# Score products of 128 keys as four products of 32 keys in column tiles

## The chip, the cores and the metric

The kernel runs on one core of one Trainium2 chip. The metric is the device time in microseconds (us) of one execution. Before the change it is 1825.35 us, the median of three runs (1824.77 to 1825.51). Engines are named as in the profile: PE is TensorE (its matmuls), PEld its weight loads, DVE is VectorE, ACT is ScalarE, POOL is GpSimd and SP is SyncE.

## The reference

The input is 32 images of 256 channels and 32 x 32 pixels, all fp32. The kernel normalises each group of 8 channels, projects to queries, keys and values (8 heads of 32 channels, 1024 tokens), computes strictly causal attention and adds the input:

```python
q = jnp.einsum('oc,bcs->bos', q_w, xf) + q_b[None, :, None]
kv = jnp.einsum('oc,bcs->bos', kv_w, xf) + kv_b[None, :, None]
k, v = (kv[:, :EMBED_C], kv[:, EMBED_C:])
...
mask = jnp.tril(jnp.ones((S, S), dtype=x.dtype), -int(MASK_CENTER))
scores = jnp.einsum('bhqd,bhkd->bhqk', q, k) / jnp.sqrt(jnp.asarray(dk, x.dtype))
scores = jnp.where(mask == 0, jnp.asarray(-10000.0, x.dtype), scores)
attn = jax.nn.softmax(scores, axis=-1)
attn = jnp.where(mask == 0, jnp.asarray(0.0, x.dtype), attn)
out = jnp.einsum('bhqk,bhkd->bhqd', attn, v)
...
x = x + _L0_conv_ref(_gn(x), L0_conv_q_w, L0_conv_q_b, L0_conv_kv_w, L0_conv_kv_b)
```

## The kernel before

Queries and keys of four heads lie in one tile with the channels on the partitions: head j of a group g has the 32 partitions 32j to 32j + 31 (`live["q", b, g]`, `live["k", b, g]`). Scores are computed transposed, keys on the PSUM partitions and queries along the columns. A product of 128 keys with up to 512 queries therefore has a stationary operand of 32 rows (channels) and 128 columns (keys), and a moving operand of 32 rows and the queries as columns. In the array it fills the row tile of its head, 32 rows by all 128 columns; the four heads lie in four row tiles.

A piece (`piece`, line 265) is one block of 128 keys against one half of the queries (512) for the four heads of a group. A piece on the diagonal is cut: with d = 1 it has two blocks, of 384 and 128 queries; with d = 2 one of 256. A long piece can also be cut into two parts of 256 queries. Each batch element has 12 visits, and a visit pairs a long piece (512 columns for each head, `full`) with a short one (256 columns for each head, `half`). There are 32 batch elements, so 384 visits.

`scores` (line 304) issues one visit. The scores go to three pairs of PSUM banks, `pairs[0]` and `pairs[1]` for heads 0, 1 and 2, 3 of the long piece, and `pairs[2]`, seen as `short`, for all four heads of the short piece, two heads in each of its banks. [...] So the short products of heads 2 and 3 come first (`first`), then the long products of heads 0 to 3, then the short products of heads 0 and 1. The last two wait on a semaphore, `bank_free`, that each product of `first` raises by one at its end; `live["free"]` holds the count to wait for. Then ACT takes three exponentials (lines 342 and 344) from PSUM to SBUF as `e` and `eh`, and POOL masks the diagonal.

`values` (line 356), one visit later, multiplies the values with `e` and `eh`: four matmuls of 128 rows and 32 columns, one for each head, that lie in four column tiles and write 32 PSUM partitions each of `acc`. The projections (`product`, line 152, called by `project_qk` and `project_v`) are cut in the same way into four column tiles of 32 columns.

The order on PE, ACT, DVE and POOL is written out by hand (`tc.manual_schedule`). The main loop (line 611) does for each visit i: the scores of visit i, what is due at i (mostly one projection, `pp` or `ppv`), the values of visit i - 1, and what is due after these (norms, row sums, results). So TensorE alternates between one stage of score products in 32x128 tiles and one stage of projections and values in 128x32 tiles.

In the trace every fp32 product stands as two loads and two matmuls (two passes): the 3584 score products are 7168 matmuls at L283. 256 visits have 8 products (16 passes), 128 have 12 (24 passes, where the long piece has blocks of 384 and 128 queries).

Of the kernel before, what the change touches and what calls it, by code (L numbers as in the profile page):

```python
# [17 lines left out]
P = 128  # L18
HD = 32
CPG = 8  # L20
HALF = 512
# [4 lines left out]
SUM_MAX = 1.0e20  # L26
HALFBANK = HALF // 2
ROW = 64


@with_exitstack
def tile_norm_attention_residual(
# [19 lines left out]
    nc = tc.nc  # L52
# [34 lines left out]
    avg = avg.rearrange("p a b -> p (a b)")  # L87
    in_range = const.tile([P, ROW], F32, name="in_range")
    nc.gpsimd.memset(in_range, 1.0)
# [8 lines left out]
    def unshifted():  # L98
        live = {}
# [178 lines left out]
        def scores_of(pc, pair, j, n=0):  # L278

            b, (g, hf, k, part, blocks) = pc  # L280
            rows = slice(HD * j, HD * (j + 1))
            kb, cols, of = blocks[n]
            return nc.tensor.matmul(  # L283
                pair[:, cols], lhsT=live["k", b, g][rows, kb * P : (kb + 1) * P],
                rhs=live["q", b, g][rows, hf * HALF + of.start : hf * HALF + of.stop],
                start=True, stop=True, skip_group_check=True,
            )

        def mask(pc, e, heads=slice(0, 4)):


            g, hf, k, part, blocks = pc
            if k < hf * BPH:
                return
            n = len(blocks)
            diagonal = e[:, heads, : n * P].rearrange("p j (n q) -> p j n q", q=P)
            nc.gpsimd.affine_select(  # L297
                out=diagonal, in_=diagonal, pattern=[[0, heads.stop - heads.start], [0, n], [1, P]],
                compare_op=ALU.is_gt, fill=0.0, base=0, channel_multiplier=-1,
            )  # L300
            if k == 0:
                nc.gpsimd.memset(e[0:1, heads, 0:1], 1.0)

        def scores(b, full, half):


            tag = "e0" if full[2] == 0 else "e"
            name = f"{b}_{full[0]}_{full[1]}_{full[2]}"
            e = epool.tile([P, 4, HALF], F32, tag=tag, bufs=4 if tag == "e0" else 3, name=f"{tag}_{name}")
            eh = epool.tile([P, 4, HALFBANK], F32, tag="eh", bufs=4, name=f"eh_{name}")  # L310
            pairs = [ps_s.tile([P, 2, HALF], F32, tag="sT", name=f"sT_{name}_{a}") for a in range(3)]
            short = pairs[2].rearrange("p bank (n q) -> p bank n q", n=2)
            last = b == B - 1 and full[:2] == (NG - 1, NH - 1) and half[2] == NB - 2
            short_of = lambda heads, n: [scores_of((b, half), short[:, j % 2, n, :], j) for j in heads]
            long_of = lambda heads, n: [scores_of((b, full), pairs[j // 2][:, j % 2, :], j, n) for j in heads]


            if not last:
                first = short_of((2, 3), 1)
                for n in range(len(full[4])):  # L320
                    long_of(range(4), n)
            else:

                long_of(range(4), 0)
                long_of((0, 1), 1)
                first = short_of((2, 3), 1)
                long_of((2, 3), 1)

            for ins in first:
                ins.then_inc(bank_free, 1)  # L330
                tc.no_tile_sem_insts.add(ins.ins.name)
            live["free"] = live.get("free", 0) + len(first)
            wait = nc.tensor.wait_ge(bank_free, live["free"])
            for ins in first:
                tc.declare_no_dep(wait.ins, ins.ins, reason="the semaphore orders them")
            for j in range(2):
                lo = scores_of((b, half), short[:, j, 0, :], j)
                for ins in first:
                    tc.declare_no_dep(lo.ins, ins.ins, reason="the semaphore orders them")
            for a in range(3):  # L340
                if a == 2:
                    exp = nc.scalar.activation(eh.rearrange("p (n bank) q -> p bank n q", n=2), short, AF.Exp)  # L342
                else:
                    nc.scalar.activation(e[:, 2 * a : 2 * a + 2, :], pairs[a], AF.Exp)  # L344

            for ins in first:
                tc.add_to_no_dep_group(f"first_{name}", ins.ins)
                tc.add_to_no_dep_group("first", ins.ins)
            tc.declare_no_dep(exp.ins, group=f"first_{name}", reason="through the last two products")
            tc.declare_fence(exp.ins, group=f"first_{name}")  # L350
            for heads in (range(2), range(2, 4)) if last else (range(4),):
                mask(full, e, slice(heads.start, heads.stop))
            mask(half, eh)
            live["e", b, full], live["e", b, half] = e, eh
# [46 lines left out]
        def sum_folded(b, heads):  # L401
            if heads.start == 0:
                live["rows", b] = small.tile([P, ROW], F32, tag="rows", name=f"rows_{b}")
            for j in heads:
# [32 lines left out]
        def check(rows, least, most):  # L437
            nc.vector.scalar_tensor_tensor(in_range, rows, least, in_range, ALU.is_ge, ALU.mult)
            nc.vector.scalar_tensor_tensor(in_range, rows, most, in_range, ALU.is_le, ALU.mult)

        def invert(b):
            rows = live["rows", b]
            check(rows, SUM_MIN, SUM_MAX)
            inv = small.tile([P, ROW], F32, tag="inv", name=f"inv_{b}")
            nc.vector.reciprocal(inv, rows)
            turned = small.tile([P, ROW], F32, tag="inv_turned", name=f"inv_turned_{b}")
            nc.vector.transpose(turned, inv)
# [94 lines left out]
        with tc.manual_schedule(engines={ENG.PE, ENG.Activation, ENG.DVE, ENG.Pool}):  # L542
# [36 lines left out]
            for b in range(B):  # L579
                first, last = b * N, b == B - 1  # L580
# [30 lines left out]
            for i in range(B * N + 1):  # L611
                if i < B * N:
                    scores(i // N, *visits[i % N])
                for f in at.pop(i, ()):
                    f()
                pcs = products[(i - 1) % N] if i else ()
                if i == B * N:

                    sums(3, pcs, False)
                for pc in pcs:  # L620
                    values((i - 1) // N, pc, i <= (B - 1) * N or pc not in by_pe)
                if i == B * N - 2:

                    sums(3, [None, *pcs])
                if i == B * N - 1:
                    sums(3, pcs)
                for f in after.pop(i, ()):
                    f()
# [172 lines left out]
```

## Time and profile before

| What | us |
|---|---|
| median of three runs | 1825.35 |
| span of the profiled execution | 1823.5 |
| PE busy with matmuls | 1811.0 (99%) |
| DVE busy | 1654.1 (91%) |
| ACT busy | 1479.1 (81%) |
| PE busy at score products, 256 columns, 3072 of 400 ns | 498.5 |
| the same, 512 columns, 2048 of 613 ns | 395.6 |
| the same, 384 columns, 1024 of 507 ns | 170.7 |
| the same, 128 columns, 1024 of 269 ns | 98.9 |
| weight loads of score products, 7168 of 184 ns | 444.3 |

The profile is of one execution. Busy time is the union of what an engine does at one time; matmuls overlap, so the rows of shapes overlap too and their sum is above what the score stages take. The means of matmuls contain the way through the array and, at the head of a stage, the wait for the first weights. A matmul's end is modelled by the profiler; its start is recorded. The granted TensorE clock is 0.998 of the full one over the span.

In a line of a group stand: source line, engine and operation, what it writes and reads, its shape (32*128 is 32 rows and 128 columns of the array, 32x256 the moving operand), how often, and then busy us and mean ns. In a line of the timeline the first two numbers are the start and the length in us of a run of such instructions. In a line of waits stand the total in us, the number of waits and the longest.

### The profile page before, as it was taken

To read this page: it belongs to the slowest core of one execution; us is meant where nothing else is said; L and a number is where in the kernel's file an instruction comes from. 1 tells how busy PE (TensorE), PEld (TensorE's weight loads), DVE (VectorE), ACT (ScalarE), POOL (GpSimd) and SP (SyncE) were. 2 spreads that over 40 slices of the span, in tenths; PEclk is the share of its full clock that TensorE was granted. 3 is DMA by queue.
4 is the path that set the end of the run, shared out by engine and by line. 5 is a ranking of instruction groups with operands and counts; after the bars stand their busy time and mean duration, and the time that the engine had idled before them with its cause. 6 is when DMAs were issued, how large, how long until landed. Compare 5 with 4: busy or idle time off the path is not lost.

```text
span 1823.5 us, 53762 instructions
## 1 busy us (share of the span) xinstructions
PE 1811.0 (99%) x23220; PEld 926.4 (51%) x23220; DVE 1654.1 (91%) x1762; ACT 1479.1 (81%) x1860; POOL 800.4 (44%) x774
## 2 busy tenths in 40 slices
PE   9999999999999999999999999999999999999997
PEld 5454555555554555555555545555455555555543
DVE  4699999999999999999999999999999999999988
ACT  6888878888788888788887888877888878888785
POOL 1553544534534445344354353443444544535432
PEclk9999999999999999999999999999999999999999
DMA  3456676676776676767767767667667676676662
GB/s 122 74 98 136 132 148 115 131 152 119 146 131 123 139 132 134 151 111 135 139 133 144 120 129 149 123 140 137 127 133 135 131 152 114 127 151 124 123 123 73
DMA packets 77780, 234.99 MB, mean 129 GB/s; under 512 B 20320, under 2 KB 21344, under 8 KB 61664
## 3 DMA queue, kind: packets, MB, share of 16 engines
q0 software_dynamic: 15872, 97.53, 39.9%
q1 hardware_dynamic: 61664, 133.96, 26.5%
q8 instruction: 183, 3.00, 0.7%
q14 instruction: 61, 0.50, 0.1%
HBM read 66.85 MB, written 34.57 MB: 56 GB/s over the span
## 4 chain that ended last, share of the span: by engine, by line
PE 99%; DVE 0%; DMA 0%; ACT 0%; issue 0%
PE sT L283 32%; PE acc L369 27%; PE pp L157 26%; PE ppv L157 13%; PE pd L414 1%; DMA x<-in_x_dram 0%; PE pv L157 0%; DVE st L167 0%; PE pm L157 0%; ACT e L344 0%; PE wt L136 0%; DVE rb_last L480 0%; ACT eh L342 0%; DVE rb_last L470 0%; DVE turned L467 0%
## 5 line engine op out<-in xcount | busy, mean ns | idle before, releaser
L344 ACT ACTIVATE e<-sT 128x1024 f32<-128x1024 f32 x768 | 744.9, 1022 | 272.9 <-PE sT L283 219.0
L377 DVE TENSOR_TENSOR e<-e,e 128x1536 f32<-128x1536 f32 x376 | 631.2, 1679 | 17.7
L377 DVE TENSOR_TENSOR e<-e,eh 128x1024 f32<-128x1024 f32 x380 | 524.3, 1394 | 117.3 <-PE acc L369 97.6
L297 POOL TENSOR_SCALAR_AFFINE_SELECT e<-e 128x512 f32<-128x512 f32 (+1 forms) x257 | 383.2, 1491 | 553.8 <-ACT e L344 550.5
L283 PE MATMUL sT<-q,k 32*128 32x256 f32 (+3 forms) x7168 | 606.4, 458 | 0.0
L283 PEld LDWEIGHTS sT<-q,k 32*128 32x128 f32 x7168 | 444.3, 184 | 153.0 <-ACT eh L342 65.0
L157 PE MATMUL pp<-xn,wT 128*32 128x512 f32 x4096 | 492.2, 598 | 0.1
L369 PE MATMUL acc<-e,v 128*32 128x512 f32 (+2 forms) x4096 | 400.6, 486 | 0.0
L342 ACT ACTIVATE eh<-sT 128x1024 f32<-128x1024 f32 x384 | 396.7, 1033 | 0.0
L393 POOL DMA_DIRECT2D e<-e x248 | 201.8, 820 | 398.0 <-DMA e<-e 318.5
L157 PE MATMUL ppv<-wT,xn 128*32 128x256 f32 x4096 | 247.5, 382 | 0.0
L369 PEld LDWEIGHTS acc<-e,v 128*32 128x32 f32 x4096 | 132.6, 110 | 223.3 <-issue 192.1
L369 PE MATMUL acc<-eh,v 128*32 128x256 f32 x3072 | 224.4, 379 | 0.0
L157 PEld LDWEIGHTS pp<-xn,wT 128*32 128x32 f32 x4096 | 107.2, 109 | 219.4 <-issue 205.7
L369 PEld LDWEIGHTS acc<-eh,v 128*32 128x32 f32 x3072 | 98.5, 110 | 164.2 <-issue 153.2
L157 PEld LDWEIGHTS ppv<-wT,xn 128*32 128x32 f32 x4096 | 120.4, 109 | 102.7 <-issue 32.4
L297 POOL TENSOR_SCALAR_AFFINE_SELECT eh<-eh 128x512 f32<-128x512 f32 x128 | 167.2, 1306 | 0.4
L223 ACT ACTIVATE xn<-x,shift,rstd 128x512 f32<-128x512 f32 x124 | 103.1, 831 | 0.0
L480 DVE SCALAR_TENSOR_TENSOR rb<-rb,v_bias_col,x 128x512 f32<-128x512 f32 x124 | 93.5, 754 | 4.4
L237 ACT ACTIVATE k<-pp,qk_bias 128x512 f32<-128x512 f32 x128 | 89.6, 700 | 2.2 <-PE pm L157 1.1
L237 ACT ACTIVATE q<-pp,qk_bias 128x512 f32<-128x512 f32 x128 | 89.8, 701 | 1.0 <-PE pp L157 1.0
L406 DVE STREAM_TRANSPOSE turned<-folded 128x512 f32<-128x512 f32 x124 | 87.6, 706 | 2.2
(70 smaller groups left out, 663.3 us busy)
## 6 DMA issues: line engine op xcount, KB each, us to landing
e<-e POOLq DMA_DIRECT2D x124, 512.0 KB, 7.0
x<-in_x_dram SPq DMA_DIRECT2D x64, 512.0 KB, 6.2
e<-e POOLq DMA_DIRECT2D x124, 256.0 KB, 4.6
folded<-e SPq DMA_DIRECT2D x124, 256.0 KB, 4.5
rb<-inverses SPq DMA_DIRECT2D x124, 256.0 KB, 8.0
out_dram<-rb SPq DMA_DIRECT2D x124, 256.0 KB, 4.5
inverses<-inv_turned SPq DMA_DIRECT2D x31, 32.0 KB, 1.7
out_dram<-rb_last SPq DMA_DIRECT2D x3, 256.0 KB, 3.4
```

Source lines behind the costliest of these rows:

```text
L157: nc.tensor.matmul(out[part], lhsT=lhsT[:, part], rhs=rhs, start=start, stop=stop, skip_group_check=True)
L223: nc.scalar.activation(xn, xt, AF.Identity, bias=live["shift", b][:, g : g + 1], scale=rstd)
L237: nc.scalar.activation(live[key][:, cols], pp, AF.Identity, bias=qk_bias[:, n, g : g + 1], scale=(SCALE, 1.0)[n],)
L283: return nc.tensor.matmul(pair[:, cols], lhsT=live["k", b, g][rows, kb * P : (kb + 1) * P], rhs=live["q", b, g][rows, hf * HALF + of.start ...
L297: nc.gpsimd.affine_select(out=diagonal, in_=diagonal, pattern=[[0, heads.stop - heads.start], [0, n], [1, P]], compare_op=ALU.is_gt, fill= ...
L342: exp = nc.scalar.activation(eh.rearrange("p (n bank) q -> p bank n q", n=2), short, AF.Exp)
L344: nc.scalar.activation(e[:, 2 * a : 2 * a + 2, :], pairs[a], AF.Exp)
L369: nc.tensor.matmul(acc[HD * j : HD * (j + 1), of], lhsT=live["v", b][:, kb, h * HD : (h + 1) * HD], rhs=e[:, j, cols], start=first, stop=l ...
L377: nc.vector.tensor_add(total[:, :, of], total[:, :, of], e[:, :, cols])
L393: nc.gpsimd.dma_start(out=total[:rows], in_=total[rows : 2 * rows], accum_op=ALU.add)
L406: nc.vector.transpose(turned, live["folded", b][:, j, :])
L480: nc.vector.scalar_tensor_tensor(rb, rb, v_bias_col[:, g : g + 1], xt[:, g, cols], ALU.add, ALU.add)
```

## The change

Each score product of 128 keys is now four products of 32 keys. The stationary operand of each has 32 rows and 32 columns, and its result goes to 32 PSUM partitions, so it lies in one 32x32 tile of the array: row tile of its head, column tile of its keys. The four read the same queries. `scores_of` returns a list of four instructions in place of one; `short_of` flattens the lists, and `long_of` doesn't use what it gets back. All eight instructions of `first` now raise `bank_free`, and the count waited for grows by eight for each visit. The order of heads is as before, with the four column tiles of a head one behind the other.

```diff
+WIDE = 32
...
             kb, cols, of = blocks[n]
-            return nc.tensor.matmul(
-                pair[:, cols], lhsT=live["k", b, g][rows, kb * P : (kb + 1) * P],
-                rhs=live["q", b, g][rows, hf * HALF + of.start : hf * HALF + of.stop],
-                start=True, stop=True, skip_group_check=True,
-            )
+            return [
+                nc.tensor.matmul(
+                    pair[c : c + WIDE, cols], lhsT=live["k", b, g][rows, kb * P + c : kb * P + c + WIDE],
+                    rhs=live["q", b, g][rows, hf * HALF + of.start : hf * HALF + of.stop],
+                    start=True, stop=True, skip_group_check=True,
+                )
+                for c in range(0, P, WIDE)
+            ]
...
-            short_of = lambda heads, n: [scores_of((b, half), short[:, j % 2, n, :], j) for j in heads]
+            short_of = lambda heads, n: [m for j in heads for m in scores_of((b, half), short[:, j % 2, n, :], j)]
...
             for j in range(2):
-                lo = scores_of((b, half), short[:, j, 0, :], j)
-                for ins in first:
-                    tc.declare_no_dep(lo.ins, ins.ins, reason="the semaphore orders them")
+                for lo in scores_of((b, half), short[:, j, 0, :], j):
+                    for ins in first:
+                        tc.declare_no_dep(lo.ins, ins.ins, reason="the semaphore orders them")
```

## The prediction

> **What bounds the kernel now.** I read the head of the page first, then the chain that ended last, the groups by shape, the timeline of TensorE round one score stage, and single instructions in narrow windows.
>
> ```profile
> span 1823.5 us, 53762 instructions
> PE 1811.0 (99%) x23220; PEld 926.4 (51%) x23220; DVE 1654.1 (91%) x1762; ACT 1479.1 (81%) x1860; POOL 800.4 (44%) x774
> PE 99%; DVE 0%; DMA 0%; ACT 0%; issue 0%
> ```
>
> TensorE is busy 99% of the span and the chain lies on it for 99%. A busy PE is not yet a full one, so the next question is whether it ever waits for another engine. Waits of PE, longest first, in the whole run:
>
> ```profile
> PE pc L497 <- DVE worst L495: 3.5, 1, 3.5
> PE busy L143 <- POOL ident masks.py:199: 1.7, 1, 1.7
> PE pm L157 <- DVE mv L168: 0.6, 1, 0.6
> ```
>
> These belong to the beginning and the end. In between TensorE follows its own order, so what one score stage gains or loses goes one to one into the span. There are 384 such stages (12 visits x 32 batches). One of them in the timeline of the matmuls and of the weight loads:
>
> ```profile
> 904.30 1.05 PE L369 MATMUL acc<-eh,v 128*32 128x256 f32 x16
> 905.27 1.57 PE L283 MATMUL sT<-q,k 32*128 32x256 f32 x16
> 906.78 1.92 PE L157 MATMUL pp<-xn,wT 128*32 128x512 f32 x16
> ...
> 905.27 1.17 PEld L283 LDWEIGHTS sT<-q,k 32*128 32x128 f32 x16 [0.41 <-issue]
> 906.78 0.16 PEld L157 LDWEIGHTS pp<-xn,wT 128*32 128x32 f32 x8 [0.33 <-issue]
> ```
>
> Eight products stand in the trace as sixteen matmuls and sixteen loads: each fp32 product runs as two passes. The stage takes 1.50 us from its first matmul to the first of the next stage. By single starts, the second passes of heads 2 and 3 begin at 905.595, row tiles 2 and 3 take their long products at 905.811 and 906.240: a pass costs 216 ns at 256 columns and 429 at 512. One row tile has a long and a short product, so 2 x 429 + 2 x 216 = 1290 ns. The rest of the 1.50 us is the first weight load, the start lag of the last tile, and 91 ns in which the tile shape changes. The same shape change costs 96 ns on the way in (the last stream of acc ends at 905.179).
>
> How long the first load shows is seen in the modelled length of a matmul right after a shape change against one later in its stage (min/median/max):
>
> ```profile
> L283 PE MATMUL sT<-q,k x2: 478/478/478, 905.3 to 905.3; 32*128 32x256 f32 x2
> L283 PE MATMUL sT<-q,k x6: 374/478/692, 905.3 to 905.6; 32*128 32x256 f32 x4, 32*128 32x512 f32 x2
> L157 PE MATMUL ppv<-wT,xn x8: 379/392/404, 901.7 to 901.9; 128*32 128x256 f32 x8
> ```
>
> 478 - 374 = 104 ns behind a load of 128 columns, 404 - 379 = 25 ns behind one of 32.
>
> The start lag is seen where four loads stand in a row (the first column is the start, 905.273 to 905.293):
>
> ```profile
> 905.27 0.20 PEld L283 LDWEIGHTS sT<-q,k 32*128 32x128 f32 x4 [0.41 <-issue]
> ```
>
> One load lasts 0.18 us and four together 0.20: tiles start 6.7 ns apart. They do so although the second pass of each product stands between them in the program, so TensorE takes work of different tiles out of order.
>
> [...] the trace has 93 (second pass of head 3 starts 905.601, ends after 374 at 905.975, the waiting load starts 906.068). [...]
>
> **The change, part by part.** It turns 3584 score products into 14336, each pass of a 32x128 tile into four of 32x32. The order of stages, the waits and all work on the other engines stay; the waits on exponentials are the same in number.
>
> Streaming: every 32x32 tile still passes the same 768 columns twice, sixteen of them at once in place of four, so 1290 ns stay. No gain here.
>
> First load: 104 ns become 25, so about -80 ns per stage. Loads in the middle are hidden behind matmuls in both.
>
> Start lag: the last of the first-started tiles is now the 16th, 15 x 6.7 = 100 ns behind the first, against 3 x 6.7 = 20 before; +80. It isn't hidden: head 1's column tile 3 must then do its long and its short product, 100 + 25 + 858 + 432 = 1415 ns, against 20 + 104 + 858 + 432 = 1414 before. These two parts cancel.
>
> The counted wait (bank_free): each visit's first products now count 8 in place of 2, and the short products of heads 0 and 1 wait behind them, with the next stage's instructions queued behind. Head 3's last tile starts 7 x 6.7 = 47 ns in, its second pass at 47 + 25 + 216 = 288, ending after 374 at 662. [...] Eight loads follow 6.7 ns apart, the last at 982, and its matmul some 30 later, 1012 (nearest row: after a real wait the mean's product loads at 7.58 and starts at 7.61). Head 1's last tile is free at 100 + 25 + 858 = 983. So +30 ns. Below: 0, if the increments run from the first completion, which is 48 ns earlier. Above: 93 / 2 = 46 ns each, 370 for eight, +127 ns. I take 30: 384 x 0.030 = 11.5 us.
>
> Stages with 24 matmuls (128 of 384, those with a block of 128 columns): now 96 passes and 96 loads. Eight tiles at a time are in such a block, one pass 107 ns, against 8 x 6.7 = 54 ns of starts, and the loads of the others come in between. I take 20 ns (0 to 107, one pass more): 128 x 0.020 = 2.6 us.
>
> Shape changes: still two per visit, 32-row tiles to 128-row tiles and back; 91 and 96 stay. Instruction fetch: 3.00 MB at 0.7% of the DMA engines, not doubling: nothing.
>
> Sum: -80 + 80 + 30 ns, 384 times, and 2.6 us: +14.1 us. The profiled execution spans 1823.5, so 1837.6. The median is 1825.35, 1.85 above that span, so 1839.5, say 1840.
>
> **The rivals.**
>
> Fed too slowly, chance 0.15. TensorE's instructions go from 46,440 to about 89,400; a visit's stage from 32 or 48 to 128 or 192. [...] In the trace before instructions come every 1811 / 46440 = 39 ns without a gap, an upper bound on the feed; the eight passes of the mean product after a real wait (16 instructions in 103 ns, 6.4 each) may have been queued. [...]
>
> Tiles not independent, chance 0.13. The trace shows overlap over four row tiles and over four column tiles, never both. If products of one column tile start in program order, a head's first pass starts with the second pass of the head before, and the stage is 4 x 429 + 4 x 216 + 216 + 45 = 2840 ns, +1.43 x 384 = 549 us: 2374.
>
> Faster, chance 0.28. Place: the first 100 ns of each stage. [...] if none of it lies on the path, 80 ns, 31 us: 1795. It decides as soon as the lag of the last tile is under 80 ns more than now and the counted wait is over by then. For it: the weight load really shrinks by 80 ns. Against it: the 6.7 ns are regular in every stage, and the wait has more increments.
>
> No change, chance 0.12: load and lag cancel and the wait stays hidden, 1825.
>
> **How the numbers follow.** My forecast, slower by about 0.8%, has 0.32; its own range is 1825 to 1825 + 127 x 0.384 + 107 x 0.128 = 1888. Below 1800 lies some 0.07 of the faster case, above 2200 the case of dependent tiles with 0.13; the range is 1800 to 2200. Within 0.2% (3.7 us) is what a measurement here can't tell from no change. Slower: 0.32 + 0.15 + 0.13 = 0.60; faster 0.28; same 0.12.
>
> **What would show it.** The stage's length from first score matmul to next stage: 1.50 now, 1.53 forecast. First matmul 399 ns long (374 + 25). Sixteen starts 6.7 ns apart. The load behind the counted wait about 935 ns into the stage. [...] if heads follow each other, tiles are dependent. A stage under 1.49 makes the forecast wrong, and so does PE waiting for exponentials.

## The result and the profile after

The changed kernel takes 2062.18 us (median of five runs, 2059.06 to 2065.94) against 1825.35 us before: a ratio of 1.13 with a 95% interval of 1.1287 to 1.1312. It is slower, as forecast, but by 13% and not by 0.8%.

The head of the page after the change, with busy time and share of the span for each engine, and the chain that ended last:

```profile
span 2064.2 us, 96826 instructions
PE 2042.5 (99%) x44724; PEld 982.8 (48%) x44724; DVE 1639.9 (79%) x1762; ACT 1488.2 (72%) x1860; POOL 745.4 (36%) x774
PE 98%; issue 1%; DVE 0%; DMA 0%; ACT 0%
```

TensorE is still the bound, and the other engines do the same work in a longer span. What PE waits for (total us, number, longest):

```profile
PE sT L285 <- issue: 9.0, 12, 1.9
PE pc L501 <- DVE worst L499: 3.5, 1, 3.5
```

No wait for exponentials has come in. The first line is new and small; it comes back at the end of this section. Now the timeline of matmuls round one stage of each kind, the smaller and the larger one (start, length, number of matmuls):

```profile
1025.80 1.97 PE L285 MATMUL sT<-q,k 32*32 32x256 f32 x64
1027.69 0.64 PE L158 MATMUL pp<-xn,wT 128*32 128x512 f32 x4
```

```profile
1041.53 2.52 PE L285 MATMUL sT<-q,k 32*32 32x256 f32 x96
1043.98 0.64 PE L158 MATMUL pp<-xn,wT 128*32 128x512 f32 x4
```

From the first score matmul to the next stage they take 1.89 and 2.45 us. Before, the smaller one took 1.50, and this is the larger one, 1.51:

```profile
937.99 1.58 PE L283 MATMUL sT<-q,k 32*128 32x256 f32 x24
939.50 0.64 PE L157 MATMUL pp<-xn,wT 128*32 128x512 f32 x4
```

From the recorded starts I worked out for all 384 stages the time from the first score matmul to the end of the last stream (the start of each matmul, plus 0.83 ns for each column: in the prediction's lines a pass of 512 columns takes 429 - 216 = 213 ns more than one of 256). After the change 355 of the 384 lie within 2 ns of the median of their kind, so one stands for all of them:

| Stages | before, ns | after, ns | number | adds up to, us |
|---|---|---|---|---|
| 8 products before | 1411 | 1807 | 256 | 101 |
| 12 products before | 1421 | 2357 | 128 | 120 |
| irregular, what they take above these medians | | | 2 before, 27 after | 19 - 1 = 18 |
| sum | | | | 239 |

The spans differ by 2064.2 - 1823.5 = 240.7 us, so all but 2 us of the loss lies inside the score stages. The shape changes around them still take 96 and 91 ns, and the projections and values are unchanged.

Inside a stage the loads tell what happens. This is the busy time by stretches of the smaller stage, of the score instructions alone (stretch, its us, PE busy with the number of matmuls, PEld busy with the number of loads, then the granted clock, the DMA share and GB/s; what overlaps a boundary counts on both sides):

```profile
1025.79:1025.95 0.16, 0.15 (x16) 0.16 (x32) 1.00 0.00 0
1026.05:1026.45 0.40, 0.40 (x33) 0.20 (x2) 1.00 0.84 164
1026.46:1026.77 0.31, 0.31 (x26) 0.30 (x15) 1.00 1.17 211
1026.92:1027.05 0.13, 0.13 (x24) 0.13 (x14) 1.00 1.30 252
```

The products of a smaller stage are numbered here in the order of the program: 1 to 8 are the short ones of heads 2 and 3, 9 to 24 the long ones of heads 0 to 3, 25 to 32 the short ones of heads 0 and 1. Which tile a record belongs to follows from this order and the times; the trace doesn't name it. Times in ns count from the first load of the stage.

In the first 0.16 us all sixteen tiles start, with both loads of each product. Then there are two loads in 0.40 us, both of product 17, and the rest stands. At 1026.47 loading goes on, but slowly, and only in the last line is it fast. In the timeline of PEld the same pause is the step from the second line to the third, each asked for in its own window:

```profile
1025.79 0.25 PEld L285 LDWEIGHTS sT<-q,k 32*32 32x32 f32 x32 [0.41 <-ACT xn L224]
```

```profile
1026.04 0.32 PEld L285 LDWEIGHTS sT<-q,k 32*32 32x32 f32 x2
```

```profile
1026.47 0.40 PEld L285 LDWEIGHTS sT<-q,k 32*32 32x32 f32 x15
```

Product 18 (long product of head 2, column tile 1) has its tile free 464 ns into the stage. Its first load comes at 672. The next seven products follow 42.6 ns apart, at 715, 757, 800, 842, 885, 927 and 970. Product 26 then stands until 1127, after which products come 16.7 ns apart. The tile of product 26 has been free since some 940. So the tiles wait for instructions that aren't there yet.

**Theory W.** A product is four instructions (load, matmul, load, matmul). Product 18, whose first load is instruction 69, loads at 672, after the modelled end of product 1 at 616; 64 instructions lie between product 1 and that load. Product 17 isn't held: its loads, instructions 65 and 67, come at 243 and 459, both before that end. So I take it that TensorE holds 64 instructions here (these times leave 64 or 65), and that their places come free in the order of the program, when an instruction and all before it have ended, not when they start. Then product 18 is let in when the four instructions of product 1 have ended, and in general product n behind product n - 17. The starts agree. Product 1's second pass starts at 242 and its modelled end is 242 + 374 = 616; product 18 loads at 672. Product 9's second pass starts at 508 and ends at 508 + 587 = 1095; product 26 loads at 1127, 32 ns later. In the larger stage products 17 to 20 end at 1261, 1502, 1545 and 1587, and products 34 to 37 load at 1292, 1533, 1575 and 1618, again 30 to 31 ns later. That a place follows the end of a matmul and not its start is seen without the modelled ends too: product 26 loads 619 ns after the start of a pass of 512 columns, product 34 of the larger stage 512 ns after one of 384. Behind product 1 it is 56 ns, and products 18 to 25, 42.6 ns apart, stand behind products 1 to 8: those are the ones that raise `bank_free`. So, says the theory, a count costs more than the wait that it is for: it holds back the place of its product.

**Rival F.** Instructions are fed too slowly, whatever they do (named in the prediction). **Rival C.** The counts alone cost the time: a semaphore is raised 3072 times and not 768.

The 27 irregular stages are up to 2 us longer than their kind. In them TensorE stands with nothing recorded that it waits for, as in this stretch of matmuls:

```profile
1507.51 1.79 PE L285 MATMUL sT<-q,k 32*32 32x256 f32 x68
1511.22 0.71 PE L285 MATMUL sT<-q,k 32*32 32x128 f32 x28 [1.92 <-issue]
```

On the larger of the two queues for instructions the DMA packets have grown from 183 to 351, and the times recorded for these packets point to late instructions. There are 18 pauses of 0.4 us or more between two starts of loads or matmuls inside score stages, and each ends 1.20 to 1.60 us after such a packet has landed, although the packets come 5.9 us apart on average. No run changes the supply of instructions alone, so this cause is likely but not shown.

### The profile page after: what moved, and what is told of

Its sections match the earlier page's. It is cut to its first block, busy times and chain, and to the rows that moved or that the text cites. A ratio compares the mean times of both kernels' runs of the same rounds, so it can differ in the third digit from the quotient of the medians.

```text
span 2064.2 us, 96826 instructions
## 1 busy us (share of the span) xinstructions
PE 2042.5 (99%) x44724; PEld 982.8 (48%) x44724; DVE 1639.9 (79%) x1762; ACT 1488.2 (72%) x1860; POOL 745.4 (36%) x774
## 4 chain that ended last, share of the span: by engine, by line
PE 98%; issue 1%; DVE 0%; DMA 0%; ACT 0%
PE sT L285 38%; PE acc L373 24%; PE pp L158 24%; PE ppv L158 12%; PE pd L418 0%; DMA x<-in_x_dram 0%; DVE st L168 0%; PE pv L158 0%; PE pm L158 0%; PE wt L137 0%; ACT e L348 0%; DVE rb_last L484 0%; ACT eh L346 0%; DVE rb_last L474 0%; DVE turned L471 0%
## 5 line engine op out<-in xcount | busy, mean ns | idle before, releaser
L285 PE MATMUL sT<-q,k 32*32 32x512 f32 (+1 forms) x28672 | 836.0, 446 | 9.3 <-issue 9.0
L381 DVE TENSOR_TENSOR e<-e,eh 128x1024 f32<-128x1024 f32 x380 | 520.9, 1385 | 361.5 <-PE acc L373 342.9
L381 DVE TENSOR_TENSOR e<-e,e 128x1536 f32<-128x1536 f32 x376 | 616.6, 1640 | 25.8 <-POOL e L301 9.0
L301 POOL TENSOR_SCALAR_AFFINE_SELECT e<-e 128x512 f32<-128x512 f32 (+1 forms) x257 | 320.6, 1247 | 838.1 <-ACT e L348 834.0
L285 PEld LDWEIGHTS sT<-q,k 32*32 32x32 f32 x28672 | 495.8, 103 | 253.6 <-ACT q L238 50.6
L386 ACT COPY num<-acc 128x512 f32<-128x512 f32 x127 | 74.5, 586 | 34.8 <-PE acc L373 30.1
```

What stands on the lines that cost most here:

```text
L285: nc.tensor.matmul(pair[c : c + WIDE, cols], lhsT=live["k", b, g][rows, kb * P + c : kb * P + c + WIDE], rhs=live["q", b, g][rows, hf * HA ...
L301: nc.gpsimd.affine_select(out=diagonal, in_=diagonal, pattern=[[0, heads.stop - heads.start], [0, n], [1, P]], compare_op=ALU.is_gt, fill= ...
L381: nc.vector.tensor_add(total[:, :, of], total[:, :, of], e[:, :, cols])
L386: nc.scalar.copy(num, acc)
```

## The experiments

**Two counts in place of eight.** Products and their order stay.

```diff
+            counted = first[P // WIDE - 1 :: P // WIDE]
             for ins in first:
-                ins.then_inc(bank_free, 1)
+                if ins in counted:
+                    ins.then_inc(bank_free, 1)
                 tc.no_tile_sem_insts.add(ins.ins.name)
-            live["free"] = live.get("free", 0) + len(first)
+            live["free"] = live.get("free", 0) + len(counted)
```

> Only column tile 3 of heads 2 and 3 raises bank_free: 2 counts a visit in place of 8; products and their order as in the changed kernel. Theory W (TensorE holds 64 instructions, one place comes free when the oldest in program order has ended, and a counted product ends its place only some 43 ns after the one before): product 18 no longer waits for eight counts in a row, but the places behind long second passes stay, so a stage of 64 passes ends about 0.12 us earlier (1.81 to 1.69) and one of 96 about 0.12 to 0.18: near 2008 us, 2000 to 2020. Rival F (instructions are fed too slowly, whatever they do): unchanged, 2062. Rival C (the counts alone cost the time): back to about 1830.

Measured: 2028.61 us, ratio 1.1121 (1.1104 to 1.1138). A smaller and a larger stage take 1680 and 2202 ns. The same stretches of a smaller stage (start of the stage 1027.08):

```profile
1027.07:1027.23 0.16, 0.15 (x16) 0.15 (x32) 1.00 0.00 0
1027.33:1027.71 0.38, 0.38 (x33) 0.21 (x3) 1.00 0.00 0
1027.72:1027.87 0.15, 0.15 (x28) 0.14 (x13) 1.00 0.00 0
```

The pause is still there, but it ends 647 ns in and not 672 (31 ns after the modelled end of product 1, now without a count; the pass that ended then had started 405 ns before, with 256 columns), and then loads come fast: 13 in 0.15 us where 15 took 0.31. By single starts products 18 to 25 load at 647, 664, 680, 723, 740, 756, 773 and 815: steps of 42.6 ns behind products 4 and 8, which still count, and of 16.7 behind the others. So a count holds its place 26 ns longer, and six of them make the 155 ns that the larger stage gains. F and C both fall as the cause of the loss in the regular stages. The regular stages gain 0.127 x 256 + 0.155 x 128 = 52 us, as W had it. The total gained 34, because the irregular stages grew to 40 with 34 us in this profile: 2028.61 lies above the 2000 to 2020 that W gave. All 27 of their pauses of 0.4 us or more end 1.18 to 1.72 us after a packet of instructions has landed. Why there are more of them stays open.

**Another order of the same products.** Of each four heads, column tile 0 of all comes first, then column tile 1 of all, and so on, except for the products behind the counted wait and the last visit.

```diff
-        def scores_of(pc, pair, j, n=0):
+        def scores_of(pc, pair, j, n=0, columns=range(0, P, WIDE)):
...
-                for c in range(0, P, WIDE)
+                for c in columns
...
-                first = short_of((2, 3), 1)
-                for n in range(len(full[4])):
-                    long_of(range(4), n)
+                first = []
+                work_of = [((b, half), short[:, j % 2, 1, :], j, 0) for j in (2, 3)]
+                for n in range(len(full[4])):
+                    work_of += [((b, full), pairs[j // 2][:, j % 2, :], j, n) for j in range(4)]
+                for i in range(0, len(work_of), 4):
+                    for c in range(0, P, WIDE):
+                        for a in range(i, min(i + 4, len(work_of))):
+                            made = scores_of(*work_of[a], columns=(c,))
+                            if a < 2:
+                                first += made
```

> The changed kernel with another order: of each four heads (2 and 3 short, 0 and 1 long; then the next four) column tile 0 of all, then column tile 1 of all, and so on. Same products, same 8 counts. Theory W: long second passes now stand among the first in program order, so the places come free later: a stage of 64 passes about 2.04 us in place of 1.81, one of 96 about 2.39 in place of 2.36, so 2062 + 0.23 x 256 + 0.03 x 128 = about 2125 us. Rivals F and C: the same number of instructions and counts, unchanged at 2062.

Measured: 2136.66 us, ratio 1.1707 (1.1686 to 1.1728); the stages take 2086 and 2500 ns. The tiles, the products and the counts are the same, and only which of them stand in front has changed. This timeline of the loads of a smaller stage shows 38 of 64, then a pause of 0.24 us in which nothing recorded is waited for, and the rest:

```profile
1006.03 0.85 PEld L285 LDWEIGHTS sT<-q,k 32*32 32x32 f32 x38 [0.41 <-ACT v L254]
1007.12 0.52 PEld L285 LDWEIGHTS sT<-q,k 32*32 32x32 f32 x26 [0.24 <-issue]
1008.21 0.16 PEld L158 LDWEIGHTS pp<-xn,wT 128*32 128x32 f32 x8 [0.57 <-issue]
```

Product 3 in this order is head 0's long one, and product 20 stands behind it. Its second pass starts 468 ns into the stage and its modelled end is 468 + 587 = 1055; products 18 and 19 load at 674 and 717, behind products 1 and 2, and product 20 loads at 1088, 33 ns after that end. A feed or a count that costs the same everywhere can't tell these orders apart. The smaller stage lost 0.28 us where 0.23 was expected, and the larger one 0.14 where 0.03 was, so my count of what stands behind what was too coarse, above all in the larger one.

**Two products of 64 keys.** `WIDE = 64`; a smaller stage has 64 instructions, a larger one 96, with four counts a visit.

> Two products of 64 keys in place of four of 32: a stage has 64 or 96 instructions in place of 128 or 192, 4 counts a visit. Theory W: 64 instructions all fit, in a stage of 96 the 65th needs the place of the first product, which has long ended when its tile is free, so nothing is held; first load some 52 ns in place of 104, start lag 7 x 6.7 = 47 in place of 20, so 25 ns a stage less than before the change: 1815 to 1825 us. Rival F: the feed is asked for half, also near 1825. Rival C: two of the six added counts are left, a third of the loss: about 1904.

Measured: 1822.73 us, ratio 0.999 (0.9983 to 0.9996). The stages take 1385 and 1426 ns. The timeline of loads in a smaller one:

```profile
1006.40 0.64 PEld L285 LDWEIGHTS sT<-q,k 32*64 32x64 f32 x24 [0.41 <-ACT eh L346]
1007.23 0.27 PEld L285 LDWEIGHTS sT<-q,k 32*64 32x64 f32 x8 [0.19 <-PE sT L285]
1007.88 0.16 PEld L158 LDWEIGHTS pp<-xn,wT 128*32 128x32 f32 x8 [0.39 <-issue]
```

All loads but those behind the counted wait come without a pause. The load behind the wait starts 826 ns into the stage, 164 after the modelled end of the last counted matmul (93 with two counts before the change), and still before its tile is free at 937. In this stage, which has no more than 64 instructions, the counts cost nothing, which speaks against C. The larger stage, which was to gain as well, is 5 ns longer than before the change. Its 96 instructions are more than the 64 of W, and by single starts its last three products, 22 to 24, load at 914, 930 and 947 ns: the first of them 31 ns after the modelled end of product 5 at 883, the others 16.7 ns apart. Their tiles come free before these weights are in, so their first matmuls last 391, 401 and 411 ns in place of 374. This is W once more; the expectation that nothing is held in a stage of 96 was wrong.

**The same with two counts.** The edit of the first experiment on top of 64 keys.

> Two products of 64 keys, and only the last of heads 2 and 3 raises bank_free, 2 counts a visit. Theory W: as with 4 counts, within 3 us, since no place is waited for. Rival C: about 80 us faster than with 4 counts, back to 1825.

Measured: 1822.38 us, ratio 0.9985 (0.9979 to 0.9992), with the same stage lengths. Two or four counts make no difference here, where two or eight made 34 us in tiles of 32. With two counts the load behind the wait starts 111 ns after the last counted end, with four 164, but it isn't what the stage waits for. As W reads it, a count costs through the place it holds.

**64 keys only where a stage fits in 64 instructions.** The larger stages go back to products of 128 keys.

```diff
-WIDE = 32
+WIDE = 64
...
+            wide = WIDE if len(full[4]) == 1 else P
...
-            long_of = lambda heads, n: [scores_of((b, full), pairs[j // 2][:, j % 2, :], j, n) for j in heads]
+            long_of = lambda heads, n: [scores_of((b, full), pairs[j // 2][:, j % 2, :], j, n, wide) for j in heads]
...
```

> Two products of 64 keys in the 256 visits whose long piece is in one block, one product of 128 keys in the 128 others. Theory W: in the first kind the stage is 1384 ns as in the run with 64 keys everywhere (1411 before the change), in the other 1421 as before, and all stages have at most 64 instructions: 0.027 x 256 = 7 us under the kernel before, 1818 us. Rivals F and C: the first kind has twice the instructions and counts of before, so no faster than before, 1825 or more.

Measured: 1819.16 us, ratio 0.9967 (0.9955 to 0.9979), stages of 1385 and 1421 ns. It beats both kernels, by 0.33% and by 12%. The timeline of matmuls shows the two kinds of stage side by side, a larger one first:

```profile
1000.65 1.58 PE L285 MATMUL sT<-q,k 32*128 32x256 f32 x24
1002.16 1.92 PE L158 MATMUL pp<-xn,wT 128*32 128x512 f32 x16
...
1005.31 1.55 PE L285 MATMUL sT<-q,k 32*64 32x256 f32 x32
1006.78 1.92 PE L158 MATMUL pp<-xn,wT 128*32 128x512 f32 x16
```

The larger one takes 1.51 us as before the change, the smaller one 1.47 against 1.50. The gain is the first load: the first matmul of a stage is 425 ns long with 64 columns, 51 above the later 374, where 128 columns had 478. The start lag takes half of it back (eight tiles, 47 ns to the last start, against 20).

## Why the prediction was wrong

What bounds the kernel was right: TensorE, with no waits, so that a stage's loss goes into the span one to one (239 of 241 us). So were the parts that were to cancel. The first matmul of a stage is 398 ns long, 24 above a later one, and 399 was forecast. Fourteen of sixteen tiles start 6.7 ns apart; the last two come 15 and 17 ns behind the one before, so the last starts 118 ns behind the first and not 100. Shape changes and streams cost what they did.

The step that failed is the one on streaming, as it was put: "every 32x32 tile still passes the same 768 columns twice, sixteen of them at once in place of four, so 1290 ns stay". At the head of the stage the sixteen tiles do work at once: all have started within 118 ns. They weren't kept full: then came two loads in 0.40 us. The step looked at what one tile has to do and not at how many instructions a stage has in flight. Before, a smaller stage had 32 and a larger one 48 of them, fewer than the 64 that W takes from the trace. After, it had 128 and 192.

In the prediction instructions that wait in TensorE come up only in the rival on the feed, as ones that "may have been queued". That each needs a place, and that a place must come free first, isn't in it. The trace after the change shows it: instruction 67 isn't held, instruction 69 is, and 64 instructions lie between it and the product whose end lets it in. That the places are given back in the order of the program and at the end, the runs showed too: product 20 in the mixed order loads 33 ns after the modelled end of product 3, and product 22 in tiles of 64 keys 31 ns after that of product 5. The feed itself takes at most the 16.7 ns in which a product of four instructions follows another once places are free, 4.2 ns an instruction. At that pace the 192 instructions of a larger stage would come in 0.80 us (192 x 4.2 ns, an estimate), and before the change the stage took 1.42. So the rival of a slow feed had the wrong cause, except perhaps in the irregular stages. Late loads within a stage can't tell it from places that are held; the experiments that left the number of instructions as it was could. And the rival of tiles that depend on each other is wrong too: the first sixteen start 6.7 to 17 ns apart, where each head was to follow the second pass of the one before.

The counted wait was given 30 ns, because its load was forecast 935 ns into the stage, with a cost for eight counts that no run had shown. It came at 970. But its price isn't in that wait. It is in the eight places, behind which loads come 42.6 ns apart in place of 16.7, and it is 127 ns in a smaller stage and 155 in a larger one with six of the eight counts gone. The stages of 24 matmuls were given 20 ns more than the others for crowded starts; they lost 936, as W reads it because 192 instructions go through 64 places three times. Instruction fetch was put at nothing because it filled 0.7% of the DMA engines; if the irregular stages come from it, as is likely, it cost 18 us.

That the direction came out right is mostly luck. The forecast had its 14 us from one wait for the counts and from crowded starts, and the loss came by another way, through the places that are held.

## What to carry to other kernels

When products are cut into smaller tiles, count the instructions that a stage needs in flight, not only the work of each tile: here a stage gained with 64, loads and both fp32 passes counted, was 5 ns longer with 96, and lost 28 and 66% of its time with 128 and 192. In a stage that needs more than that, put short matmuls in front of long ones and keep semaphore counts off the instructions at the front: here long ones in front cost 0.28 us in a smaller stage and 0.14 in a larger one, and six counts 0.127 and 0.155. Halving the width of a tile can still pay through the first weight load, as long as the stage fits: here the first matmul was 425 ns long in place of 478, and a stage of 64 instructions 1385 in place of 1411.

## What the runs showed of the hardware

- Matmuls of different tiles started out of the order of the program: before the change head 2's long product starts at 905.811, ahead of the second pass of head 0's at 905.821, which stands before it in the program. The places that W assumes came back in order: in the mixed order product 20, behind product 3 with its end at 1055 ns, loads at 1088, although the counted products 5, 6, 9, 10, 13 and 14 have ended by 702.
- With eight counts the loads of products 18 to 25 come 42.6 ns apart, each behind a product that raises the semaphore. With two counts the steps are 42.6 ns behind those two products and 16.7 behind the others.
- From the last counted matmul's modelled end to the waiting load it is 93 ns with two counts before the change. In tiles of 64 keys it is 111 with two and 164 with four, some 26 ns a count.
